# A sliding-window transformer kernel: the maximum added later in the turn, and half of v projected between keys and queries

## The chip, the cores and the metric

The kernel runs on one core of a Trainium2 chip, as one program. The metric is device time in microseconds, the median of a few executions. A core has a matrix engine (TensorE, PE in the profile), a vector engine (VectorE, DVE), an engine for activation functions (ScalarE, ACT), a general engine (GpSimd, POOL), and a queue that only issues DMAs (SyncE, SP). Each engine works through its own list of instructions in order, and semaphores hold an instruction until what it needs is there. Matmul results land in PSUM, which has eight banks of 128 x 512 fp32.

## The reference, cut to what matters

Sixteen sequences of 256 tokens with 128 channels pass through a window attention with 16 heads of 8 channels (the first part), and then through six layers, each a local attention and a feed-forward block:

```python
def attn_layer(x, Wqkv, qs, ksc, Wo):
    q, k, v = jnp.split(x @ Wqkv, 3, -1)          # 16 heads of 64 each
    q = l2norm(q) * qs; k = l2norm(k) * ksc
    q = q * cos * scale + rotate_half(q) * sin * scale
    k = k * cos / scale + rotate_half(k) * sin / scale
    out = local_attention(q, k, v)                # windows of 32, softmax over 64 keys
    return out @ Wo
...
x = attn_layer(shift_tokens(x), ...) + x
x = ffn_layer(shift_tokens(x), ...) + x           # layer norm, W1, a * gelu(gate), W2
```

## The kernel before

The first part (`first_attention`) takes two sequences at a time as a unit, eight units in all, in software-pipelined stages. Its layer-norm statistics are made by `row_stats`, once on the input (`pre == "a"`) and once behind the attention (`"b"`).

The six layers are cut into 192 tiles of 128 tokens, 32 to a layer. The main loop runs over turns. Turn `t` holds stages of different tiles, side by side: projections of tile `t` (`stage_p`), scores of tile `t - 1` (`stage_s`), injection of the maximum and the exponential of tile `t - 2` (`stage_e`), probabilities times v of tile `t - 3` (`stage_v`), the output projection of tile `t - 5` (`stage_w`), and a part of a feed-forward block of two sequences (`stage_f`). Every fourth turn begins a feed-forward block, which is spread over four turns. Each stage is a Python generator cut by `yield`; `merge_at` takes a list of places between 0 and 1 of the turn for each and runs the pieces in the order of their places. That order is the program's order, and every matmul and transpose is pinned to it (`mul`, `flip`), so PE's list is exactly this order. The lists of the other engines are put together by a scheduler, which may move instructions against one another where the data allow it.

The places in a turn are: six projections at 0, 1/6, ... 5/6; injections at `AT_E`; the two halves of probabilities times v at 0.1 and 0.45; output projection at 0.47; scores at 0.72; and the feed-forward pieces in the four turns of a block:

```python
AT_F = ((0.86,), (0.06, 0.74, 0.88), (0.03, 0.27, 0.8), (0.1, 0.35, 0.6))
```

The pieces in order: centring and square (0.86); mean, Ln, Exp, normalised input (0.06); three gate projections, each with a gelu (0.74, 0.88, 0.03 of the next turn); three projections `a`, each multiplied with the gate (0.27, 0.8, 0.1); the second weight (0.35).

A projection (`project`) is three fp16 matmuls of 128 x 512 into one bank, and between them four transposes of earlier tiles from a list `turns`: in a turn's six projections these are the keys of tile `t - 1` (kt, first two), its queries (qt, next two) and the probabilities of tile `t - 2` (pt, last two). A projection of q or k is read by DVE, which multiplies it with the rotary tables into `mc` (L656), and by ACT, which squares it into `sq` (L664); POOL adds the two halves into `sum` (L667). When both halves of q or of k are there, `norm` takes the sum of squares (DVE, L640), Ln and Exp for the inverse root (ACT, recorded at L275), a minimum (POOL, L643), and scales both halves (POOL, L646). A projection of v is copied by ACT into `vb` (L677), which has three buffers, and six or fewer DMAs bring shifted windows of it into other tiles.

PSUM is dealt out in three rings: two banks for the projections, four for transposes, feed-forward, output projection and the first half of probabilities times v, and two for scores and the second half of probabilities times v. A score bank is held from the scores to the exponential of the next turn.

The maximum of the scores is taken by DVE (`nm`, L748), and subtracted on PE: a matmul with the identity adds the negative maximum to the bank (the injection), and ACT then takes the exponential into `p`. Probabilities times v is divided on DVE (L800, L801), split into two fp16 halves by ACT and POOL (`ohl`, L805 and L806), and turned by a transposing DMA.

ACT holds one table of functions at a time. Ln and Exp are issued through `tab`, gelus through `gelu`: the first gelu of a block is made to follow every Ln or Exp issued before it, and a Ln or Exp follows the gelu last issued before it. Behind the third gelu the table that holds both Ln and Exp is preloaded (L892).

Of the kernel before, what the change touches and what calls it, by code (L numbers as in the profile page):

```python
# [14 lines left out]
AF = mybir.ActivationFunctionType  # L15
ALU = mybir.AluOpType
AX = mybir.AxisListType
# [5 lines left out]
NV = 3  # L23
# [1 line left out]
KT = 2  # L25
LAG_S, LAG_P, LAG_V, LAG_W = 1, 2, 3, 5
AT_P = tuple(c / 6 for c in range(6))
AT_E, AT_V, AT_W, AT_S = (0.09, 0.095), (0.1, 0.45), (0.47,), (0.72,)
AT_F = ((0.86,), (0.06, 0.74, 0.88), (0.03, 0.27, 0.8), (0.1, 0.35, 0.6))
AT_L = 0.71  # L30
LOAD_AT = 6
# [24 lines left out]
def kernel(  # L56
# [23 lines left out]
    V, S, G, T = nc.vector, nc.scalar, nc.gpsimd, nc.tensor  # L80
# [193 lines left out]
    def tab(*args, **how):  # L274
        made = S.activation(*args, **how)  # L275
        if opened:
            behind(made, opened[-1])
        before.append(made.ins)
# [11 lines left out]
    def mul(*args, **how):  # L290
        pin(T.matmul(*args, **how))  # L291
# [5 lines left out]
    def first_attention(p1, p2, p3, pqp, psp0, pop, pyp, ptp=None):  # L297
        ptp = ptp or pyp
        def rsqrt(dst, src, scale):
            if dst.shape[1] != 128:  # L300
                S.activation(dst, src, AF.Ln, bias=epst, scale=scale)
                S.activation(dst, dst, AF.Exp, scale=-0.5)
                return
            n = dst.shape[1]
            a = p3.tile([128, n], F32, name=f"rqa{n}")
            b = p3.tile([128, n], F32, name=f"rqb{n}")
            V.tensor_scalar(b, src, scale, EPS, ALU.mult, ALU.add)
            S.activation(a, b, AF.Ln)
            S.activation(a, a, AF.Exp, scale=-0.5)
            V.tensor_tensor(b, b, a, ALU.mult)  # L310
            V.tensor_tensor(b, b, a, ALU.mult)
            V.tensor_scalar(b, b, -0.5, 1.5, ALU.mult, ALU.add)
            V.tensor_tensor(dst, b, a, ALU.mult)

        def row_stats(xt, pre):
            mu = p3.tile([128, 4], F32, name=f"{pre}mu")
            rs = p3.tile([128, 4], F32, name=f"{pre}rs")
            sq = p3.tile([128, 128], F32, name="sq0")
            if pre == "a":
                for t in range(4):  # L320
                    S.activation(sq, xt[:, t], AF.Copy, scale=-1.0 / 128.0, accum_out=mu[:, t : t + 1])
            else:
                V.tensor_reduce(mu, xt, AX.X, ALU.add)
                G.tensor_scalar(mu, mu, -1.0 / 128.0, None, ALU.mult)
            for t in range(4):
                S.activation(sq, xt[:, t], AF.Square, bias=mu[:, t : t + 1], accum_out=rs[:, t : t + 1])
            rsqrt(rs, rs, 1.0 / 128.0)
            return mu, rs
# [39 lines left out]
        def stage_load(u):  # L368
            if u:
                load_x(u)  # L370
            e = U[u]
            _, e.rs = row_stats(e.xt, "a")
            e.rv = p1.tile([128, 4], F32, name="rv")
            G.tensor_scalar(e.rv, e.rs, VPRE, None, ALU.mult)
            yield
            e.xnt = p1.tile([128, 2, 4, 128], FR, name="xnt")
            pt = ptp.tile([128, 4, 128], F32, name="pt" if ptp is not pyp else "py")
            for t in range(4):
                T.transpose(pt[:, t], e.xt[:, t], ident)
            S.copy(e.xnt[:, 0], pt)  # L380
            V.tensor_tensor(e.xnt[:, 1], pt, e.xnt[:, 0].bitcast(F32), ALU.subtract)
            G.tensor_tensor(e.xt, e.xt, bpt.unsqueeze(1).to_broadcast([128, 4, 128]), ALU.add)
            yield
# [128 lines left out]
        def stage_norm(u):  # L512
            e = U[u]
            g, hb = divmod(u, 2)
            dma(r1d[g][:, 4 * hb : 4 * hb + 4], e.xt)
            mu, rs = row_stats(e.xt, "b")
            xn = p3.tile([128, 4, 128], F32, name="xn")
            V.tensor_tensor(mu, mu, rs, ALU.mult)
            for t in range(4):
                S.activation(xn[:, t], e.xt[:, t], AF.Identity, bias=mu[:, t : t + 1], scale=rs[:, t : t + 1])  # L520
            yield
            pt = ptp.tile([128, 4, 128], F32, name="pt" if ptp is not pyp else "py")
            for t in range(4):
                T.transpose(pt[:, t], xn[:, t], ident)
            pb = pt.rearrange("p (b j) t -> p b (j t)", j=2)
            S.copy(xg[g][0:64, 2 * hb : 2 * hb + 2, 0:256], pb[0:64])
            S.copy(xg[g][64:128, 2 * hb : 2 * hb + 2, 1:257], pb[64:128])
            yield
# [31 lines left out]
    def bank(kind):  # L560
        n = USE.get(kind, kind)
        return banks[n].tile([128, 512], F32, name=f"bank{n}")
# [14 lines left out]
    vbs = [keep.tile([128, 2, 8, 65], F32, name=f"vb{n}") for n in range(NV)]  # L577
# [27 lines left out]
    def turn(k):  # L605
        for f in turns[:k]:
            f()
        del turns[:k]
# [17 lines left out]
    def project(d, n):  # L626
        pp = bank("p")
        for q, (a, c) in enumerate(((0, 0), (0, 1), (1, 0))):
            mul(pp, d.xhl[:, a, d.j], wqs[d.i % 2][n][:, c], start=(q == 0), stop=(q == 2))
            turn(2 if q == 1 else 1)  # L630
        return pp

    def stage_p(t):
        d = tiles[t]
        tq = tqs[d.i]
        d.nat = {}
        late = []

        def norm(r, sq, mcs):
            V.tensor_reduce(r, sq, AX.X, ALU.add)  # L640
            tab(r, r, AF.Ln, bias=tiny)
            tab(r, r, AF.Exp, scale=-0.5)
            G.tensor_scalar(r, r, 1e12 / WPRE, None, ALU.min)  # L643
            for hb, mc in enumerate(mcs):
                rb = r[:, hb * 8 : hb * 8 + 8]
                G.tensor_tensor(mc, mc, rb.unsqueeze(2).to_broadcast([128, 8, 64]), ALU.mult)  # L646

        for s in (1, 0):
            r = front.tile([128, 16], F32, name="r", bufs=3)
            sq = front.tile([128, 16, 64], F32, name="sq", bufs=2)  # L650
            mcs = []
            for hb in range(2):
                pp = project(d, 2 * s + hb)
                p4 = pp.rearrange("p (h f d) -> p h f d", f=2, d=32)
                prod = front.tile([128, 8, 2, 2, 32], F32, name="mc", bufs=2)
                V.tensor_tensor(  # L656
                    prod,
                    p4.unsqueeze(3).to_broadcast([128, 8, 2, 2, 32]),
                    tq[:, s, d.j].unsqueeze(1).to_broadcast([128, 8, 2, 2, 32]),
                    ALU.mult,  # L660
                )
                mc = front.tile([128, 8, 64], F32, name="sum", bufs=NSUM)
                m2 = prod.rearrange("p h f g d -> p h f (g d)")
                S.activation(  # L664
                    sq[:, hb * 8 : hb * 8 + 8], pp.rearrange("p (h d) -> p h d", d=64), AF.Square
                )
                G.tensor_tensor(mc, m2[:, :, 0], m2[:, :, 1], ALU.add)  # L667
                mcs.append(mc)
                while late:
                    norm(*late.pop())  # L670
                yield
            late.append((r, sq, mcs))
            d.nat[s] = mcs
        d.vb = vb = vbs[t % NV]
        for hb in range(2):
            pp = project(d, 4 + hb)
            S.copy(  # L677
                vb[:, :, hb * 4 : hb * 4 + 4, 0:64],
                pp.rearrange("p (m a d) -> p a m d", a=2, d=64),
            )  # L680
            while late:
                norm(*late.pop())
            if hb == 0:
                yield
        d.v31 = work.tile([128, 8, 65], F32, name="v31", bufs=3)
        d.vw2 = work.tile([128, 8, 65], F32, name="vw2", bufs=3)
        d.vw0 = vw0[t % 4]
        dma(d.v31[64:128], vb[0:64, 1])
        dma(d.v31[0:64], vb[64:128, 0])
        for a in range(2):  # L690
            dma(d.vw2[64 * a : 64 * a + 64], vb[32:96, a])
            dma(d.vw0[64 * a : 64 * a + 32], vb[96:128, a])
            if d.j:
                dma(d.vw0[64 * a + 32 : 64 * a + 64], tiles[t - 1].vb[0:32, a])
        yield
# [216 lines left out]
    for t in range(total + 3 if LAYERS else 0):  # L912
# [8 lines left out]
        for lag, places, stage in (  # L921
            (0, AT_P, stage_p),
            (LAG_P, AT_E, stage_e),
            (LAG_V, AT_V, stage_v),
            (LAG_W, AT_W, stage_w),
            (LAG_S, AT_S, stage_s),
        ):
            if 0 <= t - lag < (total if t < total + 2 else 0):
                parts.append((places, stage(t - lag)))
# [102 lines left out]
```

## Time and profile before

| | |
|---|---|
| median of 3 executions | 3234.64 us (3232.51 to 3235.36) |
| the profiled execution | 3233.52 us, its span 3231.7 us |
| PE busy | 2969.9 us, 92% |
| DVE, ACT, POOL busy | 2559.5, 2378.0, 2536.6 us |
| first part, before the first scores of the layers | 272 us |
| table loads on ACT (L281 and L892) | 48 and 47, 1.283 us each |

A row of groups or of the timeline names the line, the engine, the operation and what it writes and reads, then busy time or start and duration, and in brackets how long the engine was idle before it and what ended that. A row of waits has the total in us, the number of times, and the longest. The granted TensorE clock is 0.57 in the first 272 us and 1.00 from there to 3178 us.

### The profile page before, as it was taken

How to read it: one execution, taken by the hardware profiler on the slowest of the kernel's cores; microseconds unless marked ns; L12 is line 12 of the kernel's file. 1: busy time of each engine (PE TensorE's matmuls, PEld its weight loads, DVE VectorE, ACT ScalarE, POOL GpSimd, SP SyncE). 2: the span in 40 equal slices, each digit the busy share in tenths (PEclk: the TensorE clock that was granted, in tenths of full speed). 3: DMA queues.
4: the chain of work that ended last, by engine and by line, in shares of the span. 5: the costliest groups of instructions: out<-in, count | busy, mean ns of one | idle time of the engine just before them, and what ended most of it. 6: DMA issues, size and time to landing. Idle time of an engine off the chain costs nothing. (4 is left out here: it accounts for less than half of the span.)

```text
span 3231.7 us, 152140 instructions
## 1 busy us (share of the span) xinstructions
PE 2969.9 (92%) x67106; PEld 2067.8 (64%) x67106; DVE 2559.5 (79%) x4306; ACT 2378.0 (74%) x4968; POOL 2536.6 (78%) x2594
## 2 busy tenths in 40 slices
PE   4778999999999999999999999999999999999997
PEld 3555666666666666666666666666666666666664
DVE  6887887887787887788787788887788888778774
ACT  7877777777777777777777777777777777777774
POOL 6768887788788778788788788788888778877872
PEclk6558999999999999999999999999999999999998
DMA  5773444444444443354444444443444444334433
GB/s 119 147 135 74 102 100 98 88 83 88 92 98 94 87 95 82 83 106 99 84 87 91 86 95 105 87 87 82 90 98 98 87 90 88 82 89 103 92 87 72
DMA packets 622935, 302.90 MB, mean 94 GB/s; under 512 B 533446, under 2 KB 545732, under 8 KB 622276
## 3 DMA queue, kind: packets, MB, share of 16 engines
q1 hardware_dynamic: 622276, 293.18, 42.6%
q8 instruction: 528, 8.65, 1.1%
q14 instruction: 131, 1.07, 0.1%
HBM read 22.45 MB, written 4.19 MB: 8 GB/s over the span
## 5 line engine op out<-in xcount | busy, mean ns | idle before, releaser
L291 PE MATMUL bank<-wqkv,xhl 128*128 128x512 f16 x3456 | 1229.9, 381 | 65.6 <-ACT sq L664 40.3
L656 DVE TENSOR_TENSOR mc<-bank,tq 128x1024 f32<-128x1024 f32 x768 | 929.0, 1221 | 185.8 <-PE bank L294 165.9
L667 POOL TENSOR_TENSOR sum<-mc 128x512 f32<-128x512 f32 x768 | 990.3, 1300 | 49.7 <-DVE mc L656 40.7
L646 POOL TENSOR_TENSOR sum<-sum,r 128x512 f32<-128x512 f32 x768 | 797.8, 1059 | 31.9
L294 PE MATMUL bank<-ident,sum 128*128 128x128 f32 x3072 | 711.2, 273 | 1.4 <-POOL sum L646 1.4
L806 POOL TENSOR_TENSOR ohl<-of,ohl 128x512 f16<-128x512 f32 x384 | 451.7, 1177 | 312.3 <-ACT ohl L805 312.1
L640 DVE TENSOR_REDUCE r<-sq 128x16 f32<-128x1024 f32 x384 | 465.2, 1211 | 168.3 <-ACT sq L664 168.2
L294 PEld LDWEIGHTS bank<-ident,sum 128*128 128x128 f32 x3072 | 432.9, 141 | 195.7 <-issue 83.4
L664 ACT ACTIVATE sq<-bank 128x512 f32<-128x512 f32 x768 | 466.6, 608 | 86.9 <-DVE mc L656 82.2
L291 PEld LDWEIGHTS <-xhl 128*128 128x128 f16 x3456 | 337.8, 98 | 177.9 <-issue 17.4
L275 ACT ACTIVATE r<-r,tiny 128x16 f32<-128x16 f32 x384 | 118.2, 308 | 398.3 <-DVE r L640 262.0
L291 PEld LDWEIGHTS bank<-vb,pt 64*32 64x32 f32 x6144 | 253.7, 105 | 164.9 <-issue 93.4
L294 PE MATMUL bank<-ident,p 128*128 128x128 f32 x1536 | 354.9, 273 | 0.7 <-issue 0.7
L805 ACT CAST ohl<-of 128x512 f16<-128x512 f32 x384 | 239.7, 624 | 150.2 <-DVE of L801 139.4
L291 PE MATMUL bank<-vb,pt 64*32 64x65 f32 x6144 | 340.8, 224 | 2.4 <-ACT pt L620 0.5
L291 PE MATMUL bank<-vw,pt 64*32 64x65 f32 x12288 | 336.7, 225 | 1.1 <-issue 1.1
L291 PE MATMUL bank<-v,pt 64*32 64x65 f32 x6144 | 315.6, 225 | 16.7 <-ACT gt L281 13.2
L291 PE MATMUL bank<-ot,wohl 128*128 128x128 f16 x4608 | 292.3, 220 | 3.2 <-DMA ot<-ohl 1.6
L801 DVE TENSOR_TENSOR of<-bank,rc 128x256 f32<-128x256 f32 x768 | 292.0, 416 | 3.2
L291 PE MATMUL bank<-kt,qt 64*32 64x64 f32 (+1 forms) x24576 | 285.1, 222 | 1.5 <-issue 1.5
L291 PEld LDWEIGHTS bank<-kt,qt 64*32 64x32 f32 x24576 | 256.6, 105 | 45.2 <-issue 45.0
L291 PEld LDWEIGHTS <-wohl 128*128 128x128 f16 x4608 | 259.3, 98 | 22.4 <-issue 3.9
(154 smaller groups left out, 5130.5 us busy)
## 6 DMA issues: line engine op xcount, KB each, us to landing
v<-vb SPq DMA_DIRECT2D x384, 130.0 KB
vw<-vb SPq DMA_DIRECT2D x384, 130.0 KB
vw<-vb SPq DMA_DIRECT2D x576, 65.0 KB
wraw<-in_L_ffn_Wqkv_dram SPq DMA_DIRECT2D x36, 256.0 KB
wraw<-in_L_ffn_Wo_dram SPq DMA_DIRECT2D x12, 256.0 KB
ot<-ohl SPq DMA_TRANSPOSE x192
xt<-in_L_attn_x_dram SPq DMA_DIRECT2D x8, 256.0 KB
r1d<-xt SPq DMA_DIRECT2D x8, 256.0 KB
```

Of the source, the lines that this page charges most:

```text
L275: made = S.activation(*args, **how)
L291: pin(T.matmul(*args, **how))
L294: pin(T.transpose(*args))
L640: V.tensor_reduce(r, sq, AX.X, ALU.add)
L646: G.tensor_tensor(mc, mc, rb.unsqueeze(2).to_broadcast([128, 8, 64]), ALU.mult)
L656: V.tensor_tensor(prod, p4.unsqueeze(3).to_broadcast([128, 8, 2, 2, 32]), tq[:, s, d.j].unsqueeze(1).to_broadcast([128, 8, 2, 2, 32]), ALU ...
L664: S.activation(sq[:, hb * 8 : hb * 8 + 8], pp.rearrange("p (h d) -> p h d", d=64), AF.Square)
L667: G.tensor_tensor(mc, m2[:, :, 0], m2[:, :, 1], ALU.add)
L801: V.tensor_tensor(of[:, :, a], po[a][:, :, 0:64], rc.unsqueeze(2).to_broadcast([128, 4, 64]), ALU.mult)
L805: S.copy(ohl[:, 0, h], of)
L806: G.tensor_tensor(ohl[:, 1, h], of, ohl[:, 0, h], ALU.subtract)
```

## The change

Three things change. The injections move from 0.09 and 0.095 to 0.20 and 0.21 of the turn, behind the first half of probabilities times v (0.1) and the second projection (1/6). The six projections of a turn come in the order k0, k1, v0, q0, q1, v1 (k0, k1, q0, q1, v0, v1 before), each half of v being copied to its half of `vb`; the norm of the keys is issued right behind v0's copy and that of the queries behind v1's, in place of behind the first q and the first v. And in the first part the statistics of the input take the mean as those behind the attention do, with one reduction on DVE and a scale on POOL in place of four accumulating copies on ACT.

```diff
-AT_E, AT_V, AT_W, AT_S = (0.09, 0.095), (0.1, 0.45), (0.47,), (0.72,)
+AT_E, AT_V, AT_W, AT_S = (0.2, 0.21), (0.1, 0.45), (0.47,), (0.72,)
...
-            if pre == "a":
-                for t in range(4):
-                    S.activation(sq, xt[:, t], AF.Copy, scale=-1.0 / 128.0, accum_out=mu[:, t : t + 1])
-            else:
-                V.tensor_reduce(mu, xt, AX.X, ALU.add)
-                G.tensor_scalar(mu, mu, -1.0 / 128.0, None, ALU.mult)
+            V.tensor_reduce(mu, xt, AX.X, ALU.add)
+            G.tensor_scalar(mu, mu, -1.0 / 128.0, None, ALU.mult)
...
-        late = []
-
...
+        d.vb = vb = vbs[t % NV]
         for s in (1, 0):
...
                 mcs.append(mc)
-                while late:
-                    norm(*late.pop())
                 yield
-            late.append((r, sq, mcs))
             d.nat[s] = mcs
-        d.vb = vb = vbs[t % NV]
-        for hb in range(2):
-            pp = project(d, 4 + hb)
+            vh = 1 - s
+            pp = project(d, 4 + vh)
             S.copy(
-                vb[:, :, hb * 4 : hb * 4 + 4, 0:64],
+                vb[:, :, vh * 4 : vh * 4 + 4, 0:64],
                 pp.rearrange("p (m a d) -> p a m d", a=2, d=64),
             )
-            while late:
-                norm(*late.pop())
-            if hb == 0:
+            norm(r, sq, mcs)
+            if s:
                 yield
```

## The prediction

> **What bounds the kernel now.** I read the page first, then the busy time of each engine in four consecutive turns, then what TensorE (PE) waited for between 300 and 3190 us, then the queues of PE and ScalarE (ACT) in one gelu turn. A turn handles one tile; a feed-forward block spreads over four turns. I cut the turns at the start of the scores (S) and call the four stretches A (the three gelus), B, C (no feed-forward work) and D (first feed-forward steps).
>
> The page, engines and slices:
>
> ```profile
> PE 2969.9 (92%) x67106; PEld 2067.8 (64%) x67106; DVE 2559.5 (79%) x4306; ACT 2378.0 (74%) x4968; POOL 2536.6 (78%) x2594
> PE   4778999999999999999999999999999999999997
> ```
>
> PE is full outside the first three slices. The four stretches A, B, C, D (start and end, length, then busy time):
>
> ```profile
> core 0: us, PE busy (x) PEld busy (x) DVE busy (x) ACT busy (x) POOL busy (x), PEclk, DMA share, GB/s
> 1781.62:1800.00 18.38, 15.69 (x340) 10.59 (x340) 12.78 (x23) 15.21 (x30) 13.62 (x15) 1.00 0.30 67
> 1800.00:1815.78 15.78, 15.78 (x340) 10.71 (x340) 14.05 (x23) 9.86 (x22) 13.96 (x15) 1.00 0.40 87
> 1815.78:1828.12 12.34, 12.22 (x327) 9.24 (x328) 10.19 (x19) 9.67 (x22) 10.07 (x12) 1.00 0.61 102
> 1828.12:1842.36 14.24, 13.97 (x332) 9.66 (x331) 10.69 (x18) 10.24 (x23) 11.38 (x11) 1.00 0.42 95
> ```
>
> B, C and D have PE busy to within 0.3 us. A alone has 2.7 us of idle PE, and there ACT is busy 15.2 of 18.4 us. Over the whole trace, from S to S, the means are 18.45, 16.02, 12.52 and 14.38, together 61.36 us, some 47 times. What PE waits for:
>
> ```profile
> PE bank L291 <- ACT gt L281: 43.9, 90, 0.8
> PE bank L291 <- ACT sq L664: 36.4, 55, 1.3
> PE bank L291 <- DVE of L801: 34.0, 80, 0.9
> PE bank L291 <- DVE gt L896: 24.1, 19, 1.3
> ```
>
> All that can be won back is here: 138 us, almost all of it in A. ACT's queue in that A:
>
> ```profile
> 1785.99 0.31 ACT L275 ACTIVATE r<-r,tiny 128x16 f32<-128x16 f32 x1 [1.35 <-DVE r L640]
> 1786.33 0.22 ACT L275 ACTIVATE r<-r 128x16 f32<-128x16 f32 x1
> 1786.56 1.28 ACT L281 ACT_TABLE_LOAD   x1
> 1787.86 0.69 ACT L281 ACTIVATE gt<-bank,b1t 128x512 f32<-128x512 f32 x1
> 1788.44 0.58 ACT L677 COPY vb<-bank 128x512 f32<-128x512 f32 x1
> ...
> 1789.69 0.71 ACT L281 ACTIVATE gt<-bank,b1t 128x512 f32<-128x512 f32 x1
> 1790.28 0.61 ACT L622 COPY kt<-bank 128x512 f32<-128x512 f32 x1
> 1790.74 0.73 ACT L281 ACTIVATE gt<-bank,b1t 128x512 f32<-128x512 f32 x1
> 1791.49 1.28 ACT L892 ACT_TABLE_LOAD   x1
> 1792.79 1.08 ACT L275 ACTIVATE p<-bank 128x512 f32<-128x512 f32 x2
> ```
>
> The query's logarithm and exponential (Ln, Exp) come just before the three gelus, so one table load leads into the group and one out of it. And PE's queue, where it feels this:
>
> ```profile
> 1782.58 0.39 PE L291 MATMUL bank<-maskb,rowsb 64*128 64x512 bf16 x1 [0.57 <-DVE of L801]
> 1788.60 0.81 PE L291 MATMUL bank<-xnhl,w1hl 128*128 128x512 f16 x3 [0.69 <-ACT gt L281]
> 1790.46 0.24 PE L291 MATMUL bank<-v,pt 64*32 64x65 f32 x1 [0.29 <-ACT gt L281]
> 1794.41 0.38 PE L291 MATMUL bank<-wqkv,xhl 128*128 128x512 f16 x1 [1.10 <-ACT sq L664]
> ```
>
> **Part 1: the front.** Per unit, four ACT copies with accumulation (L321: 0.307 us plus 0.193 to read the accumulator, 32 times, 16 us) become one VectorE (DVE) reduction and one GpSimd (POOL) scale (rows of the second statistics: 0.672 and 0.227 us, 8 times each, 7.2 us). In the first 272 us DVE is busy 209 and ACT 208, so neither is alone the bound; between -16 (all of ACT's was on the path) and +7 (all of the new) I take 0, since the removed work lies beside full DVE and the added beside full ACT.
>
> **Part 2: the order of projections.** PE's instructions keep their number and places in the turn (k0, k1, v0, q0, q1, v1 instead of k0, k1, q0, q1, v0, v1); nothing is saved there. What moves is the query's norm: its reduction, Ln and Exp are now issued after v1, at 0.833 of the turn, which lies behind the first gelu at 0.74 in turns that have one. Tables depend on order, and in the built order of the changed kernel ACT stands in each A as: square of q1, load, gelu 0, load, Ln, load, Exp, copy of v1, xhl, pt1, load, gelu 1, kt0, gelu 2, load (L892), square of k0, ohl, kt1, two exps of p. Five loads where there were two; in the program 236 for 96. The 140 new ones are 140 x 1.283 = 180 us of ACT, on an engine with 854 us free, but they stand in A.
>
> Walk of A, 0 at the start of S, with the start-to-start times of the rows (ACT: copies and squares 0.48, ohl 0.52, xhl 0.32, Ln 0.34, Exp 0.22, load 1.28 to 1.30, gelu 0.6 to 0.7, exps 0.5; DVE: products and reductions 1.14, the two maxima 1.27, an eviction's two reciprocals 0.22 and two products 0.70). ACT: product of q1 on DVE (1.14) done at 1.75 (from D below); square 2.35; load 3.63; gelu 0 4.3; load 5.6; Ln 5.9; load 7.2; Exp 7.4; v1 copy 7.9; xhl 8.2; pt1 8.7; load 10.0; gelu 1 10.7. PE: S 1.74; gelu-0 matmuls 0.65 to 2.4; v1 with its transposes 1.08 to 3.5; gelu-1 matmuls 4.15; k0 5.2; gelu-2 matmuls 5.9. The first half of P times V (V0) comes next, and its second bank is the one, four allocations back in a pool of four, that gelu 1 has to read: PE stands until 10.7, 4.8 us. Before, this same V0 went on at 8.84 (1790.46 less 1781.62), with the injections behind it. Queued behind V0 on PE is everything, k1 first; on DVE and POOL the evictions of V0.
>
> On from 10.7: V0 11.5, k1 12.6, injections 13.1, gate matmuls 13.8, v0 14.9. ACT: kt0 11.2, gelu 2 11.8, load 13.1, square 13.5, ohl 14.1, kt1 14.6, two exps 15.6. V1 reuses the two score banks, so it waits 0.75 for the exps; then V1 16.45, W (1.35) 17.8, q0 and q1 20.0, plus 0.1 for small gaps: 20.1 for 18.45, +1.65. In this are gone the S wait (0.57), the first gelu wait (0.69) and the square wait (1.10). Low end +0.45 (chain starts 0.45 earlier, as in C, and V1's wait hidden); high end +3.85, three loads with nothing regained.
>
> Page against row: the Trainium skill, "ScalarE: Activation LUTs", section "What ACT_TABLE_LOAD costs", counts a drain of about 1.38 us beside the load, 2.66 us a switch. Here gelu starts 1.30 us after the load's start, and no such drain shows, so the row decides; by the page A would be some 4.1 us longer, 195 us in all. The same page, "Table sets: the hidden batching unit", says that Ln then Exp needs one load; the built order has one before each. By the page's rule one load in three would go, some 60 us less; I go by the order.
>
> **Part 3: the injections at .20 and .21.** Before, the exps had V0, a projection and often more (4 us, 1.08 a projection) between the injections (0.53 from their first matmul to V0's) and V1. Now only v0 (1.08) lies between, in A also 0.65 and in B 2.67 of feed-forward work. And in ACT's built order kt1 and ohl (which waits for DVE's eviction of V0) stand ahead of the exps. Per stretch:
>
> C: mc of q1 1.3, square 1.9, reduction to 3.1, two maxima to 4.3, mc of k0 5.45, V0's eviction (0.22 + 0.70) 6.4, ohl 6.95, kt1 7.45, exps 8.5. PE would be at V1 at 7.4: a new wait of 1.1. All of PE's work is 11.75 (S 1.74, six projections 6.5, injections 0.53, V0 and V1 1.6, W 1.35), so 12.9 for 12.52, +0.4. Ends: -0.4 (old waits gone, none new) and +1.15.
>
> D: ACT now has Ln, Exp (after DVE's reduction, 3.7), copy, pt1 ahead of the square L866 (5.3), for which PE stands 0.5; then Ln 6.95, square, Exp 8.1, DVE's product 8.85, xnhl 9.4, kt1 9.9, exps 11.0. PE reaches V1 at 9.8, waits 1.25, ends at 15.4 for 14.38, +1.0. DVE's late evictions shift q1's product to 1.75 in A. Ends: -0.2 (S wait gone) and +1.5.
>
> B: the second bank of V0 waits for DVE's gate product behind the reduction and both maxima, 5.0 against 4.55; the exps are covered by 2.67 us of W2 matmuls. 16.2 for 16.02, +0.2; ends 0 and +0.5.
>
> DMAs: the v copies' transfers are issued after v1 as before, on the same queue, and read three turns later; the first half of v is only in SBUF sooner. No cost (uncovered it would be a landing, 5.07 us for ot in the chain of waits, against two turns, 30 us, of slack).
>
> **Sum.** 1.65 + 0.2 + 0.4 + 1.0 = 3.25 us per four turns, x 47 = 153 us. The profiled execution took 3233.5 (span 3231.7), 1.1 under the median of 3234.6; so 3388. The ends give -0.15 and +7.0 per four turns, -7 and +329 us.
>
> **Rivals.**
> 1. Only the loads cost (0.16): exps stay covered since DVE and ACT settle earlier than I walk. For it: DVE idles up to 1.4 us ahead of the query's reduction and could start the chain sooner. Then A alone, with or without V1's wait: +0.9 to +1.65, 42 to 78 us, 3277 to 3313. Against it: ohl stands ahead of the exps, and in the old C they ended 2.26 us after the first injection, where 1.6 (0.53 and 1.08) are there now.
> 2. All loads lie on the path (0.12): ACT becomes the bound through A and the backlog runs into B: 3.85 + 0.4 + 1.0 + 0.2 = 5.45, 256 us, 3490. Against it: A's old waits, 2.6 us, absorb part.
> 3. Faster (0.04): the gelus' Ln and Exp are swallowed, because gelu 0 no longer waits for the query's norm (1.35 us in ACT's row above), and the waits for DVE of (34) and ACT sq (36) and DVE gt (24) go: 3234 - 94 = 3140. It decides from where gelu 1 ends before 8.84; my walk has 10.7, so 1.9 us of the chain, one and a half loads, would have to vanish.
> 4. No change (0.02): gains and loads cancel, A's at +0.45 with C and D at their low ends.
>
> **How the numbers follow.** My forecast has 0.66. Slower by over 0.2% (6.5 us, about what these runs can tell): 0.66 + 0.16 + 0.12 = 0.94; same 0.02; faster 0.04. The range leaves out the faster and equal cases, rival 1's lower third and rival 2's upper half: 3295 to 3465.
>
> **What would show it.** Right: about 236 table loads of 1.28 us; in A the load-Ln-load-Exp row between two gelus; V0's matmuls waiting some 4 to 5 us for gt L281; bank waits at V1 for exps of p in C and D; A near 20, D near 15.4, C near 12.9; the waits for DVE of at S gone. Wrong: V0 in A starting before 9 us, or no PE wait on p in C and D; or loads that do not show 1.28 us each.

## The result, and the profile after

The changed kernel takes 3510.36 us (median of 4, 3504.74 to 3511.03) for 3234.77 before: a ratio of 1.085, 95% interval 1.0831 to 1.0868. It is 275.6 us slower, where 153 were forecast, and 45 us above the end of the range. The direction was right; the size was not.

The page of the changed kernel, engines and slices:

```profile
PE 3068.6 (87%) x67106; PEld 2123.1 (61%) x67106; DVE 2546.0 (73%) x4314; ACT 2567.3 (73%) x5044; POOL 2535.5 (72%) x2602
PE   5778988998988998988899898899898889989887
```

PE's matmuls are the same 67106, yet busy 99 us longer, and ACT is busy 189 us longer. The slices of 8 show that PE now stands through the whole kernel, not in its first part alone. The same four stretches A, B, C, D as before, of the same tiles (start and end, length, busy time, PE's granted clock):

```profile
core 0: us, PE busy (x) PEld busy (x) DVE busy (x) ACT busy (x) POOL busy (x), PEclk, DMA share, GB/s
1929.47:1950.46 20.99, 16.59 (x339) 11.32 (x340) 11.92 (x20) 18.30 (x29) 13.75 (x16) 0.92 0.26 58
1950.46:1966.70 16.24, 16.06 (x339) 10.81 (x339) 13.53 (x23) 9.66 (x20) 12.56 (x13) 1.00 0.40 85
1966.70:1979.74 13.04, 12.53 (x329) 9.31 (x328) 10.52 (x19) 9.78 (x21) 11.09 (x13) 1.00 0.56 96
1979.74:1995.27 15.53, 14.25 (x332) 9.77 (x332) 11.67 (x21) 11.36 (x24) 11.55 (x12) 1.00 0.43 88
```

Every stretch is longer: 2.61, 0.46, 0.70 and 1.29 us. In A the idle time of PE went from 2.7 to 4.4 us, and PE's busy time also rose, by 0.9 us, at a granted clock of 0.92. Over all stretches, from S to S, the means are 21.39, 16.44, 13.43 and 15.84 us, together 67.10 for 61.36. The first scores come at 279.2 us for 272.1. What PE waits for, from 300 to 3440 us:

```profile
PE bank L291 <- ACT pt L616: 126.9, 46, 2.8
PE bank L291 <- ACT gt L281: 76.8, 46, 1.7
PE bank L291 <- ACT p L275: 61.4, 187, 0.7
PE bank L291 <- ACT gt L856: 32.7, 41, 1.3
PE bank L291 <- DVE gt L886: 11.1, 41, 1.4
```

The waits for DVE's evictions (34.0) and for ACT's squares (36.4) are gone. In their place stand, 46 times, 2.8 us for the copy of pt (ACT's copy of the transposed probabilities) and 1.7 for the second gelu. ACT's queue in A shows why:

```profile
1931.80 1.28 ACT L281 ACT_TABLE_LOAD   x1
1933.09 0.69 ACT L281 ACTIVATE gt<-bank,b1t 128x512 f32<-128x512 f32 x1
1933.80 1.28 ACT L275 ACT_TABLE_LOAD   x1
1935.10 0.31 ACT L275 ACTIVATE r<-r,tiny 128x16 f32<-128x16 f32 x1
1935.42 1.28 ACT L275 ACT_TABLE_LOAD   x1
1936.71 0.21 ACT L275 ACTIVATE r<-r 128x16 f32<-128x16 f32 x1
...
1937.61 0.59 ACT L616 COPY pt<-bank 128x512 f32<-128x512 f32 x1
1938.21 1.28 ACT L281 ACT_TABLE_LOAD   x1
1939.51 0.69 ACT L281 ACTIVATE gt<-bank,b1t 128x512 f32<-128x512 f32 x1
```

From one gelu to the next there are three loads, Ln, Exp, and the copies behind them. PE in the same time:

```profile
1934.74 0.81 PE L291 MATMUL bank<-xnhl,w1hl 128*128 128x512 f16 x3
1938.25 0.30 PE L291 MATMUL bank<-vb,pt 64*32 64x65 f32 x2 [2.70 <-ACT pt L616]
1940.25 0.24 PE L291 MATMUL bank<-v,pt 64*32 64x65 f32 x1 [1.70 <-ACT gt L281]
...
1941.42 0.61 PE L291 MATMUL bank<-wqkv,xhl 128*128 128x512 f16 x1
1941.82 0.42 PE L294 MATMUL bank<-ident,sum 128*128 128x128 f32 x1
```

The first half of probabilities times v (V0) goes on at 10.78 us after S, where the walk had 10.7. What the walk lacked is in the last two lines: the projection behind the stand has matmuls of 0.61 and transposes of 0.42 us, where 0.38 and 0.27 are the rule.

### The profile page after: what moved, and what is told of

The parts are those of the page before. It is cut to its first block, busy times and chain, and to the rows that moved or that the text cites. A ratio compares the mean times of both kernels' runs of the same rounds, so it can differ in the third digit from the quotient of the medians.

```text
span 3507.6 us, 152302 instructions
## 1 busy us (share of the span) xinstructions
PE 3068.6 (87%) x67106; PEld 2123.1 (61%) x67106; DVE 2546.0 (73%) x4314; ACT 2567.3 (73%) x5044; POOL 2535.5 (72%) x2602
## 5 line engine op out<-in xcount | busy, mean ns | idle before, releaser
L291 PE MATMUL bank<-wqkv,xhl 128*128 128x512 f16 x3456 | 1274.6, 391 | 8.1 <-ACT sq L659 5.1
L294 PE MATMUL bank<-ident,sum 128*128 128x128 f32 x3072 | 735.8, 281 | 10.3 <-ACT pt L616 9.6
L294 PEld LDWEIGHTS bank<-ident,sum 128*128 128x128 f32 x3072 | 448.6, 146 | 164.5 <-issue 46.4
L291 PE MATMUL bank<-vb,pt 64*32 64x65 f32 x6144 | 387.3, 234 | 176.2 <-ACT pt L616 127.4
L291 PEld LDWEIGHTS bank<-vb,pt 64*32 64x32 f32 x6144 | 267.6, 109 | 345.2 <-ACT pt L616 150.6
L291 PE MATMUL bank<-v,pt 64*32 64x65 f32 x6144 | 326.9, 234 | 107.5 <-ACT gt L281 76.8
L637 POOL TENSOR_SCALAR r<-r 128x16 f32<-128x16 f32 x384 | 96.6, 252 | 442.9 <-ACT r L275 442.7
L790 DVE RECIPROCAL rc<-bank 128x4 f32<-128x4 f32 x768 | 94.5, 164 | 357.0 <-PE bank L291 355.1
L291 PE MATMUL bank<-vw,pt 64*32 64x65 f32 x12288 | 345.7, 235 | 1.3 <-issue 1.2
L291 PEld LDWEIGHTS bank<-v,pt 64*32 64x32 f32 x6144 | 244.8, 110 | 139.1 <-ACT gt L281 85.3
```

The source lines that it names most:

```text
L294: pin(T.transpose(*args))
```

## The experiments

Three explanations were on the table: the table loads with what PE's stand (the time in which PE waits for the second gelu) does to its clock, the late injections, and the new order of projections. The runs below take each alone, or take one away. Ratios are to runs of the kernel before on the same chip.

### 1. The injections alone

```diff
-AT_E, AT_V, AT_W, AT_S = (0.09, 0.095), (0.1, 0.45), (0.47,), (0.72,)
+AT_E, AT_V, AT_W, AT_S = (0.2, 0.21), (0.1, 0.45), (0.47,), (0.72,)
```

(in the kernel before)

> The kernel before, with nothing but the injections moved to 0.20 and 0.21 of the turn. Theory (three separate costs: the table loads in stretch A, the half clock after the long stand of PE there, and exps that come too late for the second half of probabilities times v): A keeps its two loads; C and D get a wait for the exps of 0.8 to 1.4 us each, B nothing, A at most 0.5; some 2.2 to 2.7 us per four turns, 47 times, 105 to 130 us, so 3340 to 3365 us. Rival (the table loads are all of the loss, the exps stay covered): at most 10 us more than before, 3235 to 3250 us.

Measured: 3228.59 us, ratio 0.998 (0.9971 to 0.999), so 5 us faster. The four stretches of that run:

```profile
1779.18:1796.13 16.95, 15.50 (x339) 10.64 (x339) 12.23 (x20) 14.27 (x28) 13.58 (x15) 1.00 0.32 72
1796.13:1811.98 15.85, 15.85 (x340) 10.76 (x340) 13.56 (x23) 9.78 (x21) 13.34 (x14) 1.00 0.40 87
1811.98:1825.03 13.05, 12.54 (x327) 9.35 (x327) 10.78 (x19) 9.72 (x22) 10.78 (x13) 1.00 0.58 96
1825.03:1840.17 15.14, 14.26 (x332) 9.78 (x332) 11.21 (x21) 11.28 (x24) 11.20 (x12) 1.00 0.46 90
```

C and D do lose, 0.54 and 0.82 us in the mean, by PE's waits for the exps at the second half (V1), as foreseen. But A gains 1.43 (mean 17.02), and the sum is a small gain. My theory had the loss right and missed the gain; the time came out near the rival's (3235 to 3250), 6 us below it, and for another reason than it gave.

### 2. The order of projections alone

The second part of the change, with injections and statistics as before.

> The kernel before, with the new order of projections and norms alone (injections at 0.09 and 0.095, statistics as before). Theory: five loads in each A, PE stands some 5 us ahead of the first half of probabilities times v, half clock after it: A +2.9 us, D +0.4 (the square of the feed-forward input stands behind the query's Ln and Exp), B and C about 0; 3.3 us per four turns, 155 us, so about 3390 us. Rival (the late injection makes most of the loss): 3235 to 3290 us.

Measured: 3476.1 us, ratio 1.0748 (1.0732 to 1.0764). A 21.50, B 16.24, C 13.16, D 15.53. The order alone makes 242 us of the 276, more than the 155 I expected: C and D lose 0.65 and 1.16 us without any late injection. So C and D lose through the order by other waits than through the injections. In D it is the square of the feed-forward input that is late (51.3 us in all), in C PE waits for DVE's maximum and for ACT's squares.

### 3. The changed kernel without the added loads

```diff
-AT_F = ((0.86,), (0.06, 0.74, 0.88), (0.03, 0.27, 0.8), (0.1, 0.35, 0.6))
+AT_F = ((0.86,), (0.06, 0.84, 0.88), (0.03, 0.27, 0.8), (0.1, 0.35, 0.6))
```

> The changed kernel, with the first gate projection and its gelu at 0.84 of the turn in place of 0.74, so behind the last projection and the query's norm; 98 loads in the program in place of 236. Theory: A falls from 21.4 us to 18.5 or 19, the half clock goes; B, C and D stay at 16.4, 13.4 and 15.8; 2.4 to 2.9 us less, 47 times, 113 to 136 us, so 3375 to 3400 us. Rival (it is the order of the projections in A, with its two banks, and not the loads): less than 50 us come back, 3460 us or more.

Measured: 3345.05 us, ratio 1.0345 (1.033 to 1.0361). A's mean is 17.73 us, in place of 21.39; B, C and D stay within 0.2 us (16.63, 13.41, 15.83). So 165 us of the 276 go with the three loads per block, more than the 113 to 136 expected, since A comes out below the old 18.45. The edit also moves the gate projection itself in PE's list, so the 165 holds the loads, the clock and this move; experiments 4 and 7 come at the loads in the old order, without it. The clock still fell in 11 of the 46 A's here, for 3.4 us each.

### 4. The loads alone

```diff
+            if n == 0 and not (last and final):
+                with tc.issue_after(gi.ins), tc.high_priority():
+                    S.preload_act_table_set("natural_log")
+                    S.preload_act_table_set("exp_and_others")
             if n == 2 and not (last and final):
```

(in the kernel before; the second gelu then needs its own load again)

> The kernel before, with two table loads put behind the first gelu of each block (and so a third ahead of the second gelu): the same five loads in A as the changed kernel has, and nothing else changed. Theory (the loads themselves, on ACT ahead of the second gelu, and the half clock after PE's stand): the second gelu ends 3 x 1.283 = 3.85 us later, and PE stands that long with the bank of the first half of probabilities times v, then about 1 us at the low clock: A 22 to 23.2 us, 3.6 to 4.8 us more, 47 times, 170 to 225 us, so 3405 to 3460 us; B, C and D as before. Rival (it is the place of the query's norm and the order of projections; loads alone fit into ACT's idle time): under 3300 us.

Measured: 3445.05 us, ratio 1.0651 (1.0637 to 1.0666), in the middle of the theory's range. Its A and B:

```profile
1886.47:1908.96 22.49, 16.77 (x338) 11.25 (x339) 12.78 (x23) 19.26 (x33) 13.65 (x15) 0.92 0.24 54
1908.96:1924.75 15.79, 15.79 (x339) 10.71 (x339) 14.07 (x23) 9.86 (x22) 13.98 (x15) 1.00 0.42 87
```

Three loads of 1.283 us put A's mean from 18.45 to 22.98, 4.53 us for 3.85 of loads; B, C and D do not move (15.96, 12.51, 14.40). The half clock is in the 4.53 as well, since it falls in all 46 A's here, and this run does not part the two. That ACT idles a quarter of the whole time did not spare A the loads.

### 5. One load less

The same edit with the first of the two `preload` lines only: four loads in A.

> The kernel before, with one table load put behind the first gelu of each block (and so a second ahead of the second gelu): four loads in A, in place of two before and five with three added. With three added, A went from 18.45 to 22.98, that is 4.53 for 3.85 us of loads. Theory (each load lies whole on PE's path, and the clock falls with the length of the stand): +2.57 us, and 0 to 0.7 for the clock, since PE stands some 3 us and no longer 4.4: A 21.0 to 21.7, 3356 to 3389 us; the granted clock falls in fewer periods than with three. Rival (loads cost more than linear, the first two are absorbed): under 3330 us.

Measured: 3396.73 us, ratio 1.0491 (1.0475 to 1.0507), above the range expected; A 22.02. The first two added loads cost 3.57 us, the third 0.96. So it is less than linear, the reverse of the rival, and about 1 us more than the loads arrives with the first two already. The clock falls here as well, in 45 of the 46 A's, though PE's stand is but 1.45 and 1.70 us with two matmuls between. My expectation of clearly fewer falls did not hold. The A's with 6.8 us at half clock (36 of them) have a mean of 22.13; the one A in which the clock stayed at 1.00 took 21.20, which is 2.75 more than before for 2.57 us of loads. So the extra 1 us is the clock, as far as a single A can tell. The granted clock over that stand and the projection behind it:

```profile
1872.50:1879.50 7.00, 3.85 (x74) 2.45 (x72) 0.97 (x4) 6.93 (x11) 1.89 (x2) 0.67 0.36 95
```

### 6. The clock

```diff
-            for q, (a, c) in enumerate(((0, 0), (0, 1), (1, 0))):
-                mul(pm, w1s[i % 2][:, c, t, n * 128 : n * 128 + 128], xhl[:, a], start=(q == 0), stop=(q == 2))
+            for again in range(5 if (t, n) == (1, 2) else 1):
+                for q, (a, c) in enumerate(((0, 0), (0, 1), (1, 0))):
+                    mul(pm, w1s[i % 2][:, c, t, n * 128 : n * 128 + 128], xhl[:, a], start=(q == 0), stop=(q == 2))
```

(in the changed kernel)

> The changed kernel, with the three matmuls of the third gate projection done five times over (the same result each time), so 12 more matmuls of 128 x 512, 2.6 us of PE work per feed-forward block, put into the time in which PE stands ahead of the first half of probabilities times v. Theory (the clock halves because PE is idle for some 5 us, and that costs 1.25 us and more in each A behind the stand): the clock stays at 1.00 there, the half takes 0.8 us in place of 1.26, the next projection 1.1 in place of 1.9; 60 to 75 us faster than the changed kernel in spite of 125 us more of PE work, so 3435 to 3450 us. Rival (the low clock only accompanies the stand and costs nothing): the same as the changed kernel, 3510 us, or more.

Measured: 3476.35 us, ratio 1.0751 (1.0735 to 1.0767) for 1.085 of the changed kernel: 34 us faster with 576 more matmuls. The changed kernel's first stand, the stand for the gelu with V0, and the projection behind it:

```profile
1935.40:1938.25 2.85, 0.15 (x2) 0.00 (x1) 0.73 (x1) 2.81 (x7) 1.15 (x2) 1.00 0.00 0
1938.25:1941.42 3.17, 1.47 (x65) 1.13 (x65) 0.00 (x0) 3.14 (x5) 2.99 (x4) 0.88 0.67 165
1941.42:1943.53 2.11, 2.11 (x10) 1.31 (x9) 0.97 (x4) 2.10 (x3) 0.00 (x0) 0.50 0.21 68
```

and the same three in the run with the repeated matmuls:

```profile
1910.30:1913.79 3.49, 3.40 (x17) 1.37 (x14) 1.23 (x1) 3.43 (x8) 1.14 (x2) 1.00 0.00 0
1913.79:1916.74 2.95, 1.24 (x64) 0.99 (x64) 0.00 (x0) 2.94 (x5) 2.95 (x4) 1.00 0.66 163
1916.74:1917.84 1.10, 1.10 (x13) 0.84 (x8) 0.97 (x4) 1.08 (x2) 0.05 (x1) 1.00 0.61 180
```

The eighth number of a row is the clock: 0.50 against 1.00, and the projection takes 2.11 against 1.10 us. The loss at that place is some 1.2 us (1.0 here and 0.2 in V0's matmuls); V1 then waits for the exps a little (0.1 and 0.19), which gives part of it back.

A's mean fell by 0.95 only (20.44), because the clock still fell in 14 of the 46 A's. There the single stand of 1.70 us was enough; these two rows are from one of them, the 3.41 us that hold the stand and the 3.41 us behind it:

```profile
1514.64:1518.05 3.41, 1.52 (x32) 0.63 (x38) 0.00 (x0) 3.38 (x6) 3.33 (x5) 1.00 0.49 118
1518.05:1521.46 3.41, 3.41 (x71) 2.19 (x53) 1.04 (x5) 3.38 (x6) 0.90 (x2) 0.50 0.43 113
```

These 14 A's have a mean of 21.12 us. In the other 32 the clock stayed at 1.00, and A is 20.11 us in 30 of them (mean of the 32: 20.15). Against 21.39 in the changed kernel that is 1.24 us an A, some 58 us over 47: this is what the half clock costs in the changed kernel's A, and the 34 us are what the repeated matmuls won back of it (B is 0.1 us longer in this run). The theory's size (1.25 us) holds where its condition is met; its condition was not met in a third of the blocks.

### 7. The query's norm late, in the old order

```diff
-            late.append((r, sq, mcs))
+            if s:
+                late.append((r, sq, mcs))
             d.nat[s] = mcs
         d.vb = vb = vbs[t % NV]
         for hb in range(2):
+            if hb:
+                late.append((r, sq, mcs))
```

(in the kernel before)

> The kernel before, with the query's norm alone issued behind the second half of v in place of the first; the projections keep their old order. Theory (loads and half clock in A come with the late norm, the waits in C and D with the order of the projections): A 21.4 to 22 as in the changed kernel, B, C and D as before, +3 us per four turns, 47 times, about 3375 us. Rival (the waits in C and D come with the late norm as well, since its Ln and Exp then stand ahead of the square of the feed-forward input and of the copies): another 1.8 us per four turns, 3460 us.

Measured: 3395.12 us, ratio 1.0492 (1.0478 to 1.0507). A 22.00, B 15.93, C 12.52, D 14.39. A as the theory had it for the changed kernel (there it is 21.39), the others as before: the theory, 20 us above its time. The loads come from where the norm is issued; the waits in B, C and D come from the order of the projections.

### 8. The order without loads and without late injections

The changed kernel with the gelu at 0.84 and the injections at 0.09 and 0.095.

> The changed kernel, with the first gate projection at 0.84 of the turn, so that the table loads are as before, and the injections at 0.09 and 0.095: the new order of projections and the statistics, without loads and without the late injection. Theory (the order itself costs B 0.2, C 0.65, D 1.16, as in the run of the order alone; A, without the added loads, is at 17.7 to 18.4; the statistics cost 7 us): 1.3 to 2 us per four turns and 7, 3305 to 3335 us. Rival (the waits in B, C and D follow from the long A): 3242 us, or less.

Measured: 3326.0 us, ratio 1.0277 (1.0263 to 1.0291), within the theory's range. A 18.25, B 16.15, C 13.17, D 15.53. What PE waits for in it:

```profile
PE bank L291 <- ACT sq L659: 69.1, 88, 1.2
PE bank L291 <- ACT gt L856: 54.0, 44, 1.8
PE bank L291 <- ACT gt L281: 45.8, 88, 0.8
PE bank L291 <- ACT pt L616: 28.0, 44, 0.7
PE bank L291 <- DVE nm L738: 18.2, 61, 0.6
```

L856, the square of the feed-forward input, was 8.1 us before; it now stands on ACT behind the query's Ln and Exp, and costs D 1.2 us each time. Of the added waits on the exps (p) there are none here; they come with the late injections.

### 9. The statistics alone

> The kernel before, with the statistics of the first part's input made by one DVE reduction and one POOL scale alone. Theory (neither ACT nor DVE is alone the bound in the first 272 us): within 3 us of the kernel before, first scores at 270 to 275 us. Rival (the reduction stands in DVE's full queue): the whole 7 us more, 3241 us, first scores at 279 us as in the changed kernel.

Measured: 3242.62 us (11 runs), ratio 1.0022 (1.0013 to 1.0031): 7.8 us, most of it ahead of the layers (first scores at 278.8 us for 272.1). The rival holds. ACT is busy 16 us less in the first 272 us, which brings nothing. The new reduction in DVE's list, as a group:

```profile
L319 DVE TENSOR_REDUCE amu<-xt 128x4 f32<-128x512 f32 x8 | 5.5, 683 | 8.3 <-DMA xt<-in_L_attn_x_dram 8.3
```

DVE stands 8.3 us in front of it for the load of the input; the first reduction had been on ACT, and DVE's list did not wait for it. That this stand is the 7.8 us is read off the trace; no run took it away.

### 10. A faster kernel: late injections in some turns

The gain of A in experiment 1 could be made in the turn of A or in the one ahead of it. Three runs place the late injections by turn:

```diff
-AT_E, AT_V, AT_W, AT_S = (0.09, 0.095), (0.1, 0.45), (0.47,), (0.72,)
+AT_E, AT_V, AT_W, AT_S = ((0.09, 0.095), (0.2, 0.21), (0.2, 0.21), (0.09, 0.095)), (0.1, 0.45), (0.47,), (0.72,)
...
-            (LAG_P, AT_E, stage_e),
+            (LAG_P, AT_E[t % 4], stage_e),
```

(shown for the turns that end D and A; the others have the late pair in one place)

In the turn that ends A alone:

> The kernel before, with the injections at 0.20 and 0.21 only in the turn that follows the first two gelus (every fourth turn, the one that ends stretch A), and at 0.09 and 0.095 in the others. With all turns late, A went from 18.45 to 17.02 us, but C from 12.52 to 13.06 and D from 14.38 to 15.20. Theory (gain and losses belong to their own turns): A 17.0, B, C and D as before, -1.4 us per four turns, 47 times, about 3168 us. Rival (the gain in A is only passed on to the next stretches): 3225 to 3235 us.

Measured: 3223.3 us, ratio 0.9965 (0.9953 to 0.9978), A 18.37. The theory fails: the gain was not made there. PE still waited 0.57 us at the start of A for DVE's evictions.

In the turn that ends D alone:

> The kernel before, with the injections at 0.20 and 0.21 only in the turn that ends D. Theory (A gains by what D's turn does to DVE's and ACT's queues, and its own late place adds nothing, since alone it gave 0.08): A 17.1, D 15.2, together 60.8, about 3209 us. Rival (both are needed: the wait at the start of A goes, and the wait of the projection for ACT's squares, 1.10, takes its place): A 17.6 to 18, sum 61.3 to 61.7, 3235 to 3250 us.

Measured: 3223.6 us, ratio 0.9959 (0.9946 to 0.9971). A 17.20, D 15.29, sum 61.04. A as the theory had it; the sum did not fall as far, with B (16.02) and C as before, and the 1.10 us for ACT's squares still in 26 of the A's. Neither account is quite right.

In both turns:

> The kernel before, with the injections at 0.20 and 0.21 in two turns of four, those that end D and A, and at 0.09 and 0.095 in the other two. With the late place in the turn of A alone, A stayed at 18.37 us and began with the old wait of the scores for DVE's evictions (0.57), so the gain seen with all turns late was not made there. Theory (the late injection in D takes that wait away at the start of A, and costs D a wait for exps): A 17.0, D 15.2, B 16.0, C 12.5, together 60.7 for 61.36, 47 times, -31 us, so about 3204 us. Rival (the gain needs C late as well): 3225 to 3235 us.

Measured: 3210.89 us, ratio 0.9921 (0.9909 to 0.9934), A 17.01, B 15.92, C 12.56, D 15.25, sum 60.73. It is 25 us faster than the kernel before and 299 faster than the changed one. Its A and D:

```profile
1770.38:1787.32 16.94, 15.51 (x340) 10.64 (x340) 12.23 (x20) 14.26 (x28) 13.59 (x15) 1.00 0.32 72
...
1815.45:1830.58 15.13, 14.25 (x331) 9.77 (x331) 11.67 (x21) 11.27 (x25) 11.86 (x13) 1.00 0.40 90
```

D pays 0.9 us for the exps, and A loses both the wait for DVE's evictions at its start and, later, the one for ACT's squares.

### The sum

| step | us |
|---|---|
| the added loads with the clock (3510.4 less 3345.1), of which the clock some 58 (experiment 6) | 165 |
| the order of projections without loads (3326.0 less 3236.4, less the statistics) | 82 |
| the late injections in that order (3345.1 less 3326.0) | 19 |
| the statistics | 8 |
| together | 274 |
| measured | 276 |

The first four rows are steps from one run to the next, so their sum is bound to come out, but for the two medians of the kernel before (3236.4 and 3234.8); it is no test of the parts. The tests are that the loads give 160 us in the old order too (experiment 7), and that the order gives 242 us with its loads (experiment 2) for 165 and 82 here.

## Why the prediction was wrong, by its own steps

The miss is some 122 us: about 60 in A, 56 in B, C and D, and 7 to 8 in the front.

**What bounds the kernel, and that it gets slower.** Right: PE was full outside A, so each new wait adds to the time. The 140 loads of 1.28 us came, at the places named, and V0 went on at 10.78 us for 10.7. The waits for DVE's evictions and for ACT's squares went, as the walk of A had them go. The DMAs of v cost nothing: none of PE's waits names them.

**Part 2, A: +1.65, measured +2.94.** The failed step is "On from 10.7: V0 11.5, k1 12.6". It takes the durations of a PE that has not stood. After the stand the matmuls run at half the clock: the rest of V0 took 1.1 to 1.3 us, where the walk had 0.80 (0.8 to 1.0 at the full clock of experiment 6), and the projection 1.8 to 2.1 for 1.08. In 30 of the 46 A's the low clock lasted 6.8 us, and the injections and the gate matmuls ran slow as well (mean 21.76 us); in 16 it lasted 3.4 us (mean 20.72). A's whole miss is 1.29 us a period, some 60 us, and the clock accounts for 1.24 of it: where experiment 6 kept the clock at 1.00, A takes 20.11 us for the walk's 20.1, W begins at 16.50 for 16.45 and q0 at 17.85 for 17.8. So the loads, the stand and the path behind it were walked rightly; what was put at nothing without a reason is the speed of PE behind its stand. The stand itself came in two parts, 2.70 us for pt and 1.70 for the gelu, where the walk had one of 4.8 for the gelu.

The trace of before could not show the price in the layers, where the granted clock was 1.00 throughout; but its first 272 us, at 0.57, did show that the clock moves, and I let that row pass. The Trainium skill, "TensorE: Matmul & The Clock Gate", section "Why this matters for your kernels", warns of idle gaps of more than about 3 us between matmuls, after which the clock is halved. That was the rule that spoke against this change, and the prediction did not weigh it. The measurement is stricter than the page: stands of 2.70 and 1.70 us, parted by two matmuls, brought the 0.50, and in experiment 6 a single 1.70 us did so in 14 of 46 blocks.

**The rule that was weighed.** For the table load the row held against the page named in the prediction (the Trainium skill, "ScalarE: Activation LUTs", section "What ACT_TABLE_LOAD costs"): at the page's 2.66 us a switch three loads would have cost 8 us in A, an estimate, and they cost 4.5 with the clock (experiment 4).

**Parts 2 and 3, B, C and D: +0.2, +0.4, +1.0, measured +0.42, +0.91, +1.46.** The walks themselves were good: 16.2, 12.9 and 15.4 us, where the stretches shown above have 16.24, 13.04 and 15.53. The failed step is the subtraction, "12.9 for 12.52", "15.4 for 14.38", "16.2 for 16.02". A walk of a stretch without weight loading was set against the mean of all, about half of which share ACT and DVE with the conversion of the next layer's weights. Against the stretches that I had shown myself (15.78, 12.34, 14.24) the same walks give 0.42, 0.56 and 1.16, 25 us more in all; the turns that load weights lost more (D there 16.54 for 14.69, where the one shown has 15.53 for 14.24).

**Part 3's cause.** "Only v0 now lies between" was taken as the reason of the waits in C and D. It is one of two. The late injections alone do bring the waits for the exps (experiment 1: C +0.54, D +0.82), but the new order alone costs C and D more than that with the old injections, by other waits (experiment 2: +0.65 and +1.16). Both together cost less than the sum (+0.91 and +1.46). And taken alone the late injections are a small gain, because A gets 1.43 us shorter: the part costed only the stretches that lose.

**Part 1: 0, measured 7 to 8.** The high end. "The removed work lies beside full DVE" was no reason for zero, since what counts is what the added instruction waits for in its list.

**The rivals.** Rival 2 (3490, given 0.12) came nearest in time. Its mechanism, a backlog of ACT that runs into B, did not: in experiment 4 the loads leave B, C and D where they were. The range was too narrow for the chances it was drawn from: it stops at 3465, below rival 2's one price of 3490, although it is said to leave out only that rival's upper half. The sum's own upper end, +329 us or 3564, covers the result.

## What to carry to other kernels

Before moving a Ln or Exp, look at which table its engine holds at the new place; in a group of gelus each foreign function cost its own loads, about in full, where the matrix engine waited for the group. When a walk finds that the matrix engine will stand, cost what comes behind the stand at half its clock as well; here stands of under 2 us were enough for it. Set a walk against the very stretch it was walked from, never against a mean that holds other work; and where a change moves a wait, cost the turns that gain as carefully as those that lose.

## What was not expected of the hardware

Added matmuls made the kernel faster. With 2.6 us more of PE work in the stand of each block the clock stayed at 1.00 in 32 of 46 blocks, the projection behind took 1.10 us in place of 2.11, and the kernel 34 us less. The granted clock fell too when PE stood for 1.45 and 1.70 us with two short matmuls between (0.67 over the 7 us of stand and projection).

In the traces of experiment 6 and of the changed kernel the clock's changes in the layers lie on a grid of 3.41 us. In experiment 6 each of the 14 falls follows a step of this grid in which PE was busy 1.52 to 1.76 us, and every step at full clock with less than 1.71 is followed by one; in the changed kernel the 46 falls follow steps with 0.30 to 1.31 us, and none follows a step with 1.54 or more. So it seems to be the busy share of such a step, and not the length of one gap, that decides; the same 1.70 us of standing then brings the half clock or not by where it lies on the grid. No run moved a stand along the grid, and in other runs the border lies a little elsewhere (falls behind up to 1.94 us in experiment 3), so this is a reading of the traces and not a rule.
